# One DMA queue, known semaphores and chunk-wise stores in a scan kernel with a planned instruction order

## The chip, the cores and the metric

The kernel runs on one core of a Trainium2 chip. Its engines run side by side, each through its own list of instructions in order: TensorE (PE, with its weight loads as PEld), VectorE (DVE), ScalarE (ACT), GpSimd (POOL) and SyncE (SP), which computes nothing and here issues transfers. Engines wait for each other, and for transfers, by semaphores. The metric is the time of one execution on the device in microseconds (us); lower is better. Changes of about half a per cent can be told from none.

## The reference

The reference is a network of two blocks on an input of shape (4, 384, 32, 32). Each block is a state-space scan with projections, followed by a feed-forward part; the second one is a mixture of four experts, two of them per token. What matters here is the scan, and the vectors dt and dt u that it needs. For the first block:

```python
dts = jnp.einsum('bkrl,kdr->bkdl', dts, dt_projs_weight)
A = -jnp.exp(A_logs.astype(jnp.float32)).reshape(K, D, N)
dt = jax.nn.softplus(dts.astype(jnp.float32) + dt_projs_bias.astype(jnp.float32)[None, :, :, None])
...
def step(h, inp):
    dtt, ut, bt, ct = inp
    dA = jnp.exp(dtt[..., None] * A)
    h = h * dA + (dtt * ut)[..., None] * bt[:, :, None, :]
    y = jnp.einsum('bkdn,bkn->bkd', h, ct)
    return (h, y)
```

The second block has the same recurrence over 768 channels in one direction, with a convolution ahead of it and a gate behind it.

## The kernel before

**Passes, parts and steps.** The scans are cut into 48 passes: 32 of the first block (an image, a direction, a half of its 1024 positions), 16 of the second (an image, a half of the positions, a half of the channels). A pass has 384 channels and 512 positions. It has three parts of 128 channels, and a part has four steps `m`, each of which holds four of the 16 states: the 128 partitions are 32 channels by 4 states, and four tiles `x` of a step cover the part's channels. One step is: ScalarE makes the decays `da` = exp(dt A) (L1784, four instructions), GpSimd makes `s` = dt u times B for all four tiles (L1778), VectorE runs the four scans (L1793) and multiplies by C (L1842; a share of it goes to GpSimd, L1858), TensorE adds over the states into `acc` (L1814), and after each part VectorE adds `acc` into the output (`gather`, L666 to L672 and L918).

**How dt reaches its layout.** `prep_pass` (L522) makes dt and dt u of a whole pass as [128 channels, 3 chunks, 512 positions]: a matmul with `dtw` (L529), a softplus on ScalarE (L540 to L560), a sum on TensorE (L553) or VectorE (L562), and a multiply by u on GpSimd (L568). `spread_out` (L511) stores the result into a DRAM buffer in four transfers, a quarter of the partitions each, for all three chunks together: once for dt after its last chunk, once for dt u after its last chunk, 384 transfers of 192 KB in all, all on SyncE's queue. `spread_pass` (L575) loads it back for each part with each row repeated over four partitions: dt u in one load of 1024 KB (L590, on SyncE's queue, two buffers `dtus`) and dt in two loads of 512 KB (L596, on ScalarE's queue, three buffers `dts`). The second half of a part's dt goes into the buffer that the first half of the part before held, so it can be issued only when the decays of that part's last step on tiles 0 and 1 are done. `bt` and `ct` hold the rows of B and C repeated over the partitions (L1775, SyncE's queue); these rows come from DRAM buffers that `rows_out` (L491, ScalarE's queue, L494) writes.

**How a new quad starts.** Two passes share one projection, a quad. `ask_quad0` (L648) loads its small weights `wx0` and `dtw` (L651, L652) as soon as the preparation of an earlier pass that uses `dtw` is over; `prep_quad0` (L627) projects on TensorE (L637), ScalarE copies the result to `xd` (L642), and the rows for B and C are stored.

**What sets the order.** Nothing is scheduled by the compiler. A planner in the kernel (`Plan`, `Lane`, `Op`) goes through the work with estimated costs and writes the instructions out in the order of its own clock. The scans and what belongs to each step are fixed streams (`Op`); all else runs in lanes, generators that yield (engine, cost) and get the time at which it will be done. A lane's next request is ready when the one before it is done, unless it names another time. A transfer's cost is its estimated time to land, `land(kb)`; SyncE itself counts as occupied for 0.1 us by each. A transfer that is issued on ScalarE's queue takes 0.55 us of ScalarE in the plan (L595) or nothing (L494, L869). Lanes have ranks; passes come first, the experts last. Decisions of `choose` (L1951) also set how many of a step's multiplies by C VectorE leaves to GpSimd. The chip then runs each engine's list in the order written, with real waits.

**Semaphores of transfers.** The transfers of SyncE and ScalarE take eight semaphores in turn, in the order in which they are written out, whichever queue they go to. Before a transfer is issued, the one before it on the same semaphore must have landed. The planner does not know of this.

**The rest.** The gate's values `z` of the second block are stored from ScalarE's queue (L869) and loaded back (L929). The experts' weights stream through SyncE's queue into `mw` (L1355, 384 KB each), and the experts' matmuls (L1420, L1442) run on TensorE between the other work once tokens are routed (L1201). The last tokens are routed after the last scan, so that expert blocks are also what the kernel ends with.

Of the kernel before, what the change touches and what calls it, by code (L numbers as in the profile page):

```python
# [133 lines left out]

class Lane:
# [18 lines left out]
    def ready(self):  # L154
        return max(self.want[2] if len(self.want) > 2 else self.end, self.floor) + SLACK[self.rank >= LOW][self.want[0]]
# [11 lines left out]
class Plan:  # L167
# [39 lines left out]
    def mains(self, e):  # L207

        out = []
        for k in range(len(self.streams.get(e, ()))):  # L210
            op = self.head(e, k)
            if op is not None and all(d in self.end for d in op.deps):
                t = max([self.end[d] + LAG for d in op.deps], default=0.0) + op.lag
                out.append((max(self.free[e], t), k, op))
        return out
# [18 lines left out]
    def run(self):  # L234
        while True:
# [22 lines left out]
            start, what, e = best  # L258
            self.stuck = max(self.stuck, start)
# [4 lines left out]
            if isinstance(what, Lane):  # L264
                cost = what.want[1]
                self.free[e] = start + (0.1 if e == SP else cost - PITCH[e])
                what.end = start + cost - SOON[e]
                what.want = None
                Free.clock = what.end
                what.go(what.end, start)  # L270
            else:
                k, op = what
                self.at[e, k] += 1
                self.free[e] = start + (0.1 if e == SP else op.cost - PITCH[e])
                self.end[op.key] = start + op.cost - SOON[e]
                op.emit()


@with_exitstack
def layers(ctx, tc, ins, out, const):  # L280
# [160 lines left out]

    def layernorm(src, dst, eps, sq=None, sq_at=0.0, centred=False, scaled=True):
# [41 lines left out]
    def wload(src):  # L484

        w = yield from wts.take()
        yield SP, land(192) + 2.5
        nc.sync.dma_start(out=w.rearrange("p c m -> p (c m)"), in_=src)
        return w

    def rows_out(q, to):  # L491

        q["rows"] = q.get("rows") or dram.tile([2 * NS, L], F32, tag="rows", name="rows", bufs=4)
        nc.scalar.dma_start(out=q["rows"][:, to], in_=xd[q["at"] : q["at"] + 2 * NS, to])  # L494
# [12 lines left out]
    def load_dtw(q, k):  # L507

        nc.sync.dma_start(out=dtw[dt_rows(q), :], in_=ins["w_dt1"][:, k * D : (k + 1) * D])

    def spread_out(to, of):  # L511

        for q in range(NG):
            nc.sync.dma_start(out=to[:, :, q, :].rearrange("c r t -> r c t"), in_=of[q * QP : (q + 1) * QP])
# [5 lines left out]
    def prep_pass(v, p, of_u):  # L520
# [25 lines left out]
        if sums_on_pe(v):  # L546
            yield ACT, 1.5
            nc.scalar.activation(dtu, dtu, AF.Ln, bias=1.0)
            for c in range(NC):
                pd = yield from ps.take(True)  # L550
                yield PE, 2.0
                nc.tensor.matmul(pd, lhsT=ident, rhs=dt[:, c, :], start=True, stop=False)
                nc.tensor.matmul(pd, lhsT=ident, rhs=dtu[:, c, :], start=False, stop=True)  # L553
                yield ACT, 0.6
                nc.scalar.copy(dt[:, c, :], pd)
                ps.give(pd)
        for c in () if sums_on_pe(v) else range(NC):
# [6 lines left out]
        spread_out(spread[0], dt)  # L564
        for c in range(NC):
            yield POOL, 1.3 if len(of_u(dt[:, c, :], c)) == 1 else 1.75
            for (to, u), (by, _) in zip(of_u(dtu[:, c, :], c), of_u(dt[:, c, :], c)):
                nc.gpsimd.tensor_tensor(to, by, u[:, c], ALU.mult)  # L568
        tmp.give(dt)
        t = yield SP, land(768)  # L570
        spread_out(spread[1], dtu)
# [3 lines left out]
    def spread_pass(p):  # L575
# [3 lines left out]
        def gen():  # L579
            spread, stored = st.pop(("spread", p))  # L580
            for part in range(NC):
# [8 lines left out]
                nc.sync.dma_start(out=dtus[n % 2].rearrange("p q t -> p (q t)"), in_=of(1, 0, NG))  # L590
                plan.end["dtu", p, part] = plan.now + land(1024)
                for x in range(2):
                    m = 2 * n + x - 3
                    before = (yield from until(("da", 4 * (m // 2) + 3, 2 * (m % 2) + 1))) if m >= 0 else 0.0
                    yield ACT, 0.55, max(before, stored)  # L595
                    nc.scalar.dma_start(out=dts[(2 * n + x) % 3].rearrange("p q t -> p (q t)"), in_=of(0, 2 * x, 2))  # L596
# [5 lines left out]
    def prep0(b):  # L602
        u = st[("u0", b)]

        def ln(h):
            def gen():
                yield SP, land(768)
                nc.sync.dma_start(out=u[h], in_=half(x_in[b], h))
# [20 lines left out]
    def prep_quad0(q, b, k):  # L629
        def gen():  # L630
# [9 lines left out]
            for h in range(NT):  # L640
                yield ACT, 0.6
                nc.scalar.copy(xd[q["at"] : q["at"] + QROW + R0, cols(h)], px[h * HP : h * HP + QROW + R0])  # L642
            rows_out(q, slice(0, L))
            ps.give(px)
# [3 lines left out]
    def ask_quad0(q, k):  # L648
        def gen():
            yield SP, land(66)  # L650
            nc.sync.dma_start(out=wx0.rearrange("p c m -> p (c m)"), in_=ins["w_x0"][k])  # L651
            nc.sync.dma_start(out=dtw[dt_rows(q), :], in_=ins["w_dt0"][k])  # L652
# [21 lines left out]
    def post0(b, h):  # L674
# [15 lines left out]
        def add_x(c):  # L690
            def gen():
                xh = yield from t1.take()
                yield SP, land(256)
                nc.sync.dma_start(out=xh, in_=piece(x_in[b], c, h))
# [8 lines left out]
        def ln2():  # L703
# [8 lines left out]
            nc.sync.dma_start(out=fold[:, :, :32], in_=fold_d)  # L712
# [14 lines left out]
        def ffn(lane):  # L727
            def gen():
# [6 lines left out]
                for i in range(2 * lane, 2 * lane + 2):  # L735
                    w, proj1 = yield from wts.two()
                    yield SP, land(192) + 2.0
                    nc.sync.dma_start(
                        out=w.rearrange("p a m -> p (a m)")[zrow, :], in_=ins["w_fc1"][:, i * NC * P : (i + 1) * NC * P]
                    )  # L740
                    nc.sync.dma_start(
# [29 lines left out]
        def ffn_out():  # L771
# [4 lines left out]
            nc.sync.dma_start(out=spread.rearrange("p a m -> p (a m)"), in_=of)  # L776
# [12 lines left out]
            nc.sync.dma_start(out=half(x1[b], h), in_=y)  # L789
# [11 lines left out]
    def prep1(b, h):  # L801
# [6 lines left out]
        def conv(i):  # L808
            def gen():
                for j in range(NC):  # L810
# [8 lines left out]
                    nc.sync.dma_start(out=dg, in_=taps_d[c])  # L819
# [33 lines left out]
        def gate(i):  # L853
            def gen():
# [14 lines left out]
                nc.scalar.dma_start(out=to.rearrange("(c p) t -> p c t", p=P), in_=z)  # L869
# [16 lines left out]
    def prep_quad1(q, b, h):  # L886
        def gen():
# [3 lines left out]
            nc.sync.dma_start(out=wx1, in_=ins["w_x1"].rearrange("p (c m) -> p c m", c=NI))  # L891
# [12 lines left out]
            nc.scalar.copy(xd[q["at"] : q["at"] + QROW + R1, cols(h)], px[: QROW + R1])  # L904
            rows_out(q, cols(h))
            ps.give(px)
# [13 lines left out]
    def post1(b, h, early=False):  # L920
# [3 lines left out]
        def gate(i):  # L924
            def gen():
# [3 lines left out]
                nc.sync.dma_start(out=z, in_=of.rearrange("(c p) t -> p c t", p=P))  # L929
# [14 lines left out]
        def project():  # L944
            o = st["o", b, h] = yield from tmp.take()
            for m in range(NC):
                w = yield from wts.two()
                yield SP, land(384)
                for i in range(2):
                    nc.sync.dma_start(out=w[i], in_=w_out[m, :, i * NC : (i + 1) * NC])  # L950
# [20 lines left out]
        def add_x(m):  # L971
            def gen():
# [3 lines left out]
                nc.sync.dma_start(out=xh, in_=piece(x1[b], m, h))  # L976
# [12 lines left out]
        def end():  # L989
            o = st["o", b, h]  # L990
            t = yield SP, STORE
            nc.sync.dma_start(out=x2[b, h].rearrange("(c p) t -> p c t", p=P), in_=o)
# [16 lines left out]
    def centre():  # L1009
# [9 lines left out]
        for c in range(NI):  # L1019
# [7 lines left out]
            nc.sync.dma_start(out=taps_d[c], in_=dg)  # L1027
            t1.give(dg)
        plan.end["taps",] = plan.now
        for i in range(2):  # L1030
# [4 lines left out]
            nc.sync.dma_start(out=w, in_=ins["w_out"][i * D : (i + 1) * D].rearrange("(c p) m -> p c m", p=P))  # L1035
# [8 lines left out]
            for m in range(NC):  # L1044
                nc.sync.dma_start(out=out_d[m, :, i * NC : (i + 1) * NC], in_=w[:, :, m * P : (m + 1) * P])
            tmp.give(t)

    def zero():
# [4 lines left out]
        for slot in (*slot_x, *slot_y):  # L1053
            for x in range(slot.shape[0] // P // n):
                to = slot.rearrange("(n p) d -> p n d", p=P)[:, n * x : n * (x + 1), :]
                yield SP, 12.0
                nc.sync.dma_start(out=to, in_=rep(z[:, :D], n))
# [265 lines left out]
    def experts():  # L1323
# [21 lines left out]
        def weights():  # L1345

            for s, i in every:
# [4 lines left out]
                for q in range(2 * NQ):  # L1352
                    w = yield from mws.take()
                    yield SP, 0.1
                    nc.sync.dma_start(out=w, in_=of[q])  # L1355
                    wq.append((plan.now + land(393) + 1.0, w))

        def fetch():

            for n, (s, i) in enumerate(every):  # L1360
# [11 lines left out]
                nc.sync.dma_start(  # L1372
# [3 lines left out]
                nc.sync.dma_start(  # L1376
# [115 lines left out]
        def keep():  # L1492

            for s0, _ in every:
# [16 lines left out]
                for k in range(m):  # L1511
                    yield SP, land(192)
                    nc.sync.dma_start(out=slot_y[g % 3][bass.DynSlice(at + k * P, P)], in_=rows[k][:, :D])
# [6 lines left out]
    def combine(u):  # L1520
# [4 lines left out]
        def begin():  # L1525
            x = st["out", u] = yield from tmp.take()
            yield SP, land(768)
            nc.sync.dma_start(out=x, in_=x2[u].rearrange("(c p) t -> p c t", p=P))

        def some(j):  # L1530
            def gen():
# [10 lines left out]
                nc.sync.dma_start(out=b2, in_=ins["b2"])  # L1542
# [30 lines left out]
        def end():  # L1573
# [3 lines left out]
            nc.sync.dma_start(out=to, in_=x)  # L1577
# [3 lines left out]
        def early():  # L1581
# [3 lines left out]
            nc.sync.dma_start(out=b2[:NE, :D], in_=ins["b2"])  # L1585
# [9 lines left out]
        def by_rows(j):  # L1595
            def gen():
# [32 lines left out]
                nc.sync.dma_start(out=to, in_=part)  # L1629
# [143 lines left out]
    def load(p, m, of, to):  # L1773
        rows = passes[p]["q"]["rows"][of + 4 * m : of + 4 * m + 4, cols(passes[p]["h"])]
        nc.sync.dma_start(out=to[m], in_=rows.unsqueeze(0).to_broadcast([QP, 4, T]))  # L1775
# [211 lines left out]

    plan = Plan(
# [10 lines left out]
def land(kb):  # L1999

    return 3.5 + kb / 200
# [105 lines left out]
```

## Time and profile before

| what | value |
|---|---|
| three runs, median (lowest to highest) | 5049.6 us (5034.54 to 5051.74) |
| the profiled execution, its own time | 5032.81 us |
| its span in the profile | 5031.0 us |
| granted TensorE clock, mean | 0.894 |
| PE busy | 4262.9 us (85%) |
| DVE busy | 4159.0 us (83%) |
| ACT busy | 3037.3 us (60%) |
| POOL busy | 4006.4 us (80%) |
| moved by DMA | 899.33 MB, 179 GB/s |
| queue q1, the larger of the two hardware queues | 704.28 MB, 43.3% of 16 engines |
| queue q10, the smaller one | 166.22 MB, 9.7% |

The profile is one execution. Busy time counts an engine's computing instructions; the issue of a transfer and the wait for a semaphore are not busy time, but they stand in the timeline as instructions of the sequencer, named SPq or ACTq. A busy TensorE is not one at its peak, since matmuls are pipelined; 751.5 us of its busy time are small matmuls by zero (L1833) that the planner puts into its gaps. The idle time before an instruction is given with what ended it: "<-ACT da L1784" says that the last thing waited for was ScalarE's instruction of line 1784 that writes `da`.

### The profile page before, as it was taken

The numbers are of one execution on the slowest core, as the hardware profiler recorded it, in microseconds if no ns is written. First come the engines' busy times: TensorE is split into PE (matmuls) and PEld (weight loads), VectorE is DVE, ScalarE is ACT, GpSimd is POOL, SyncE is SP. The second block draws the span as 40 slices with busy tenths as digits, with TensorE's granted clock in tenths as the row PEclk, the third lists the DMA queues.
The fourth block names the chain that finished last, engine by engine and source line by source line (L and its number), as shares of the span: only waits on it lengthen the run. The fifth ranks groups of instructions, "written<-read, shape, count | busy, mean of one in ns | idle before, by whom it ended". The sixth has DMA issues, their size and how long they took to land. (4 is left out here: it accounts for less than half of the span.)

```text
span 5031.0 us, 57132 instructions
## 1 busy us (share of the span) xinstructions
PE 4262.9 (85%) x17967; PEld 2192.9 (44%) x17967; DVE 4159.0 (83%) x5754; ACT 3037.3 (60%) x4769; POOL 4006.4 (80%) x1826
## 2 busy tenths in 40 slices
PE   8777778887767799988877798899888888899999
PEld 3222222222223454444444454345534333569996
DVE  4999999999999899999989999999999999850002
ACT  4544458765545577767654577767685756554442
POOL 2999999999988898989988988889899988850002
PEclk9887889888888899999987899899988889899998
DMA  4344656654443565556564655466655454655556
GB/s 148 110 161 156 205 169 214 207 185 139 161 143 107 195 193 175 190 188 211 188 221 161 215 181 175 155 197 205 230 179 191 155 181 148 220 184 180 170 165 190
DMA packets 394191, 899.33 MB, mean 179 GB/s; under 512 B 62384, under 2 KB 143520, under 8 KB 375456
## 3 DMA queue, kind: packets, MB, share of 16 engines
q1 hardware_dynamic: 336672, 704.28, 43.3%
q10 hardware_dynamic: 49024, 166.22, 9.7%
q0 software_dynamic: 8192, 25.17, 1.6%
q8 instruction: 143, 2.34, 0.2%
q14 instruction: 160, 1.31, 0.1%
HBM read 712.11 MB, written 183.40 MB: 178 GB/s over the span
## 5 line engine op out<-in xcount | busy, mean ns | idle before, releaser
L1778 POOL TENSOR_TENSOR s<-dtus,bt 128x2048 f32<-128x2048 f32 x576 | 2605.3, 4533 | 178.1 <-PE acc L1814 67.2
L1784 ACT ACTIVATE da<-dts,a 128x512 f32<-128x512 f32 x2304 | 1530.2, 686 | 886.4 <-DVE s L1842 771.5
L1814 PE MATMUL acc<-s,four 128*32 128x512 f32 x4608 | 735.1, 682 | 382.0 <-POOL s L1858 344.9
L1858 POOL TENSOR_TENSOR s<-s,ct 128x512 f32<-128x512 f32 (+1 forms) x552 | 942.5, 1708 | 138.6 <-DVE s L1793 102.0
L1793 DVE TENSOR_TENSOR_SCAN da<-da,s 128x512 f32<-128x512 f32 x775 | 918.2, 1216 | 114.0 <-ACT da L1784 82.4
L1842 DVE TENSOR_TENSOR s<-da,ct 128x512 f32<-128x512 f32 x1529 | 1009.6, 680 | 0.1
L1793 DVE TENSOR_TENSOR_SCAN da<-da,state,s 128x512 f32<-128x512 f32 x754 | 939.5, 1277 | 17.7 <-ACT da L1784 10.1
L1833 PE MATMUL acc<-ident,few 128*32 128x256 f32 x2886 | 751.5, 416 | 36.2 <-DVE big L918 18.6
L1833 PEld LDWEIGHTS acc<-ident,few 128*32 128x32 f32 x2886 | 334.4, 119 | 510.6 <-issue 225.1
L1793 DVE TENSOR_TENSOR_SCAN s<-da,state,s 128x512 f32<-128x512 f32 x398 | 495.5, 1267 | 8.7 <-ACT da L1784 8.6
L1793 DVE TENSOR_TENSOR_SCAN s<-da,s 128x512 f32<-128x512 f32 x377 | 447.1, 1204 | 17.3 <-ACT da L1784 17.3
L1814 PEld LDWEIGHTS acc<-s,four 128*32 128x32 f32 x4608 | 106.5, 113 | 748.9 <-POOL s L1858 547.3
L1420 PE MATMUL ps<-tmp,mw 128*128 128x256 f32 (+1 forms) x1812 | 387.9, 369 | 22.3 <-ACT tmp L1465 11.5
L1442 PE MATMUL ps<-mw,tmp 128*128 128x192 f32 x2096 | 377.1, 337 | 17.5 <-DMA mw<-in_w_dram 6.8
L1442 PEld LDWEIGHTS ps<-mw,tmp 128*128 128x128 f32 x2096 | 350.4, 195 | 82.4 <-issue 42.9
L1420 PEld LDWEIGHTS ps<-tmp,mw 128*128 128x128 f32 x1812 | 316.5, 198 | 135.7 <-issue 30.4
L1615 DVE SCALAR_TENSOR_TENSOR big<-big,gk,da 128x384 f32<-128x384 f32 x2 | 1.2, 612 | 414.2 <-PE da L1613 414.2
L1605 POOL DMA_INDIRECT big<-ys,slot x12 | 11.8, 980 | 382.7 <-DMA ys<-t 379.3
L799 PE MATMUL ps<-big,w 128*128 128x512 f32 x576 | 280.2, 627 | 14.3 <-DMA w<-in_w_in_dram 8.2
L568 POOL TENSOR_TENSOR tmp<-tmp,big 128x256 f32<-128x256 f32 (+1 forms) x186 | 193.0, 1063 | 68.3 <-DVE tmp L1037 68.3
L529 PE MATMUL ps<-xd,dtw 12*128 12x512 f32 (+1 forms) x288 | 187.9, 743 | 17.2 <-ACT tmp L542 9.4
L838 PE MATMUL ps<-tmp,t 128*128 128x512 f32 x368 | 175.3, 620 | 15.6 <-ACT tmp L830 9.9
(448 smaller groups left out, 5322.2 us busy)
## 6 DMA issues: line engine op xcount, KB each, us to landing
mw<-in_w_dram SPq DMA_DIRECT2D x414, 384.0 KB
dts<-dts ACTq DMA_DIRECT2D x288, 512.0 KB
dtus<-dts SPq DMA_DIRECT2D x144, 1024.0 KB
dts<-tmp SPq DMA_DIRECT2D x376, 192.0 KB
bt<-rows SPq DMA_DIRECT2D x192, 256.0 KB
ct<-rows SPq DMA_DIRECT2D x192, 256.0 KB
dts<-in_w_dram SPq DMA_DIRECT2D x78, 384.0 KB
ys<-t SPq DMA_DIRECT2D x32, 768.0 KB
```

What stands on the lines that cost most here:

```text
L529: nc.tensor.matmul(pd, lhsT=dtw[dt_rows(q), c * P : (c + 1) * P], rhs=xd[dt_rows(q), cols(h)], start=True, stop=True,)
L568: nc.gpsimd.tensor_tensor(to, by, u[:, c], ALU.mult)
L799: nc.tensor.matmul(pi, lhsT=w[:, c, :], rhs=u[:, c], start=c == 0, stop=c == NC - 1)
L1420: nc.tensor.matmul(ph[:, k * width : (k + 1) * width], lhsT=w[:, c, k * P : (k + 1) * P], rhs=turned[:, c], start=c == 0, stop=c == NC - 1,)
L1442: nc.tensor.matmul(py[:, k * HD : (k + 1) * HD], lhsT=by_f(hids[half_], width)[:, at_, k * P : (k + 1) * P], rhs=w[:, f], start=4 * q + f ...
L1778: nc.gpsimd.tensor_tensor(ss[i % NSR], dtus[part_of(i) % 2], rep(bts[i % 4], NG), ALU.mult)
L1784: nc.scalar.activation(das[x], dts[(2 * part_of(i) + x // 2) % 3][:, x % 2, :], AF.Exp, scale=v["a"][:, g, m : m + 1])
L1793: nc.vector.tensor_tensor_scan(d if in_psum else s, d, s, 0.0 if v["first"] else state[:, v["slot"], j, x : x + 1], ALU.mult, ALU.add)
L1814: nc.tensor.matmul(acc[x * QP : (x + 1) * QP, :], lhsT=four, rhs=ss[i % NSR][:, x, :], start=m == 0, stop=m == 3)
L1833: nc.tensor.matmul(acc[:QP, : 2 * P], lhsT=nil.to_broadcast([P, QP]), rhs=rep(ident, 2), start=fresh, stop=fresh)
L1842: nc.vector.tensor_tensor(ss[i % NSR][:, x, :], das[x], cts[i % 4], ALU.mult)
L1858: nc.gpsimd.tensor_tensor(s[:, m:, :], s[:, m:, :], rep(cts[i % 4], NG - m), ALU.mult)
```

## The change

All transfers of SyncE and ScalarE go through SyncE's queue. Each is written out by a helper `ask`, which tells a new class `Ring` of its size. `Ring` keeps the time at which each of the eight semaphores will be free and the time at which the queue's data will have moved, at 220 KB per us; the planner lets SyncE start a transfer no earlier than the next semaphore is free, and counts SyncE as occupied for 0.55 us by each. `land(kb)` goes from 3.5 + kb/200 to 3.2 + kb/220. Transfers that were written on ScalarE's queue become steps of their lanes on SyncE, with their landing time as cost. `spread_out` stores one chunk of 128 channels (256 KB) in one transfer, and `prep_pass` calls it for each chunk as soon as dt or dt u of that chunk is made: 288 transfers of 256 KB in place of 384 of 192 KB. Where a store's step stands inside the lane of `prep_pass`, the lane's next request is ready when the store is estimated to have landed.

```diff
+class Ring:
+    at = busy = 0.0
+    lands = [0.0] * 8
+    n = 0
...
+    @classmethod
+    def next(cls):
+        return cls.lands[cls.n % 8] + 0.1
+
+    @classmethod
+    def issue(cls, kb):
+
+        t = max(cls.at, cls.next())
+        cls.busy = max(t + 1.2, cls.busy) + kb / RATE
+        cls.lands[cls.n % 8] = cls.busy + 1.0
+        cls.n += 1
+        cls.at = t + ISSUE
...
     def ready(self):
-        return max(self.want[2] if len(self.want) > 2 else self.end, self.floor) + SLACK[self.rank >= LOW][self.want[0]]
+        least = Ring.next() - LAG if self.want[0] == SP or len(self.want) > 3 else 0.0
+        return max(self.want[2] if len(self.want) > 2 else self.end, self.floor, least) + SLACK[self.rank >= LOW][self.want[0]]
...
-                out.append((max(self.free[e], t), k, op))
+                out.append((max(self.free[e], t, Ring.next() if e == SP else 0.0), k, op))
...
             start, what, e = best
+            Ring.at = start
...
                 what.go(what.end, start)
+                self.free[e] = max(self.free[e], Ring.at) if Ring.at > start else self.free[e]
...
                 op.emit()
+                if e == SP:
+                    self.free[e] = max(self.free[e], Ring.at)
...
+    def ask(queue, out, in_):
+
+        Ring.issue(int(np.prod(out.shape)) / 256)
+        queue.dma_start(out=out, in_=in_)
...
     def rows_out(q, to):
...
-        nc.scalar.dma_start(out=q["rows"][:, to], in_=xd[q["at"] : q["at"] + 2 * NS, to])
+        ask(nc.sync, out=q["rows"][:, to], in_=xd[q["at"] : q["at"] + 2 * NS, to])
...
-    def spread_out(to, of):
-
-        for q in range(NG):
-            nc.sync.dma_start(out=to[:, :, q, :].rearrange("c r t -> r c t"), in_=of[q * QP : (q + 1) * QP])
+    def spread_out(to, of, c):
+
+        ask(nc.sync, out=to[c].rearrange("r q t -> q r t"), in_=of[:, c])
...
                 nc.scalar.copy(dt[:, c, :], pd)
                 ps.give(pd)
+                yield SP, land(256)
+                spread_out(spread[0], dt, c)
...
             nc.vector.tensor_tensor(dt[:, c, :], dt[:, c, :], pd, ALU.add)
             ps.give(pd)
-        spread_out(spread[0], dt)
+            made = plan.free[DVE]
+            yield SP, land(256), made
+            spread_out(spread[0], dt, c)
...
                 nc.gpsimd.tensor_tensor(to, by, u[:, c], ALU.mult)
+            t = yield SP, land(256)
+            spread_out(spread[1], dtu, c)
         tmp.give(dt)
-        t = yield SP, land(768)
-        spread_out(spread[1], dtu)
         tmp.give(dtu)
...
-                    yield ACT, 0.55, max(before, stored)
-                    nc.scalar.dma_start(out=dts[(2 * n + x) % 3].rearrange("p q t -> p (q t)"), in_=of(0, 2 * x, 2))
+                    yield SP, land(512), max(before, stored)
+                    ask(nc.sync, out=dts[(2 * n + x) % 3].rearrange("p q t -> p (q t)"), in_=of(0, 2 * x, 2))
...
-                nc.scalar.dma_start(out=to.rearrange("(c p) t -> p c t", p=P), in_=z)
+                yield SP, land(768)
+                ask(nc.sync, out=to.rearrange("(c p) t -> p c t", p=P), in_=z)
...
+            ps.give(px)
+            yield SP, land(64)
             rows_out(q, cols(h))
-            ps.give(px)
...
 def land(kb):
 
-    return 3.5 + kb / 200
+    return 3.2 + kb / 220
+
+
+RATE, ISSUE = 220.0, 0.55
```

Every other `nc.sync.dma_start(...)` of the planned part becomes `ask(nc.sync, ...)` with the same operands.

## The prediction

> **What bounds the kernel now.** I read the stages first: busy time of each engine from the first scan (99.4 us) to the last (4478 us), and behind it. The columns are PE, PEld, DVE, ACT, POOL busy us, granted clock, DMA share, GB/s.
>
> ```profile
> 99.40:4478.00 4378.60, 3627.08 (x14812) 1691.00 (x14813) 4082.93 (x5460) 2767.76 (x4313) 3951.45 (x1769) 0.88 0.54 179
> 4478.00:5031.00 553.00, 545.63 (x2869) 465.17 (x2868) 43.11 (x126) 223.38 (x379) 44.41 (x44) 0.96 0.59 179
> ```
>
> In the first stage VectorE works 4083 of 4379 us: 296 us of idle time is all that a change in waiting can win there. In the last 553 us TensorE works without a gap on expert blocks whose tokens are routed late, so this stage moves with the first one as a whole. No transfer goes through ScalarE's queue there; I cost it at nothing (bounds -5 and +33 us, one block of 33 us more or less in the backlog).
>
> Then the waits, for who holds VectorE up and who stands behind that (total us, times, longest):
>
> ```profile
> ACT xd L642 <- PE ps L637: 106.8, 14, 15.7
> PE ps L637 <- DMA wx<-in_w_x_dram: 93.8, 12, 14.9
> DVE da L1793 <- ACT da L1784: 92.5, 39, 14.1
> ...
> DVE s L1793 <- ACT da L1784: 25.8, 13, 5.9
> ```
>
> The first two rows are one chain: the small weight `wx` (L651) lands late, the projection L637 stands first in TensorE's order and waits, ScalarE waits for its result and cannot make the decays behind it. The worst case, SyncE's timeline:
>
> ```profile
> 1662.24 0.54 SPq L1775 DMA_DIRECT2D bt<-rows  x1
> 1662.89 0.58 SPq L1775 DMA_DIRECT2D ct<-rows  x1
> 1663.53 0.59 SPq L590 DMA_DIRECT2D dtus<-dts  x1
> 1664.21 8.83 SPq L514 DMA_DIRECT2D dts<-tmp  x4
> 1673.09 0.43 SPq L651 DMA_DIRECT2D wx<-in_w_x_dram  x1
> ```
>
> and VectorE's line at the end of that chain:
>
> ```profile
> 1683.57 2.35 DVE L1793 TENSOR_TENSOR_SCAN da<-da,s 128x512 f32<-128x512 f32 x2 [14.12 <-ACT da L1784]
> ```
>
> The four quarter stores of dt u need 8.83 us although an issue takes 0.43: of the four, the third and the last wait, the last for 5.2 us, until the semaphore that a dts load from ScalarE's queue holds is free. Over the first stage I find 64 such waits of SyncE, 158 us, of which 132 us (46 waits) are for a dts load of ScalarE.
>
> **The change, part by part.** All times are on the profiled execution: 5032.8 us its own time, 5031.0 its span. Landings are read from the semaphores: the last increment before the semaphore's next transfer is issued.
>
> (a) *The wx chain.* Ten times a gap of VectorE ends a chain from L637: 4.8, 6.2, 9.9, 7.6, 5.9, 7.8, 14.1, 8.3, 7.3 and 5.0 us, 77 us together. Before these wx issues the trace shows 31 us of waits for a semaphore of ScalarE's loads, which the new order does not have, since semaphores are then taken in one queue's order and the eighth transfer back is some 20 us old (about 1800 transfers in 4379 us). One chunk store instead of four quarters ahead of wx saves 3 issues of 0.43 us each time, 13 us. The rest is GpSimd's multiply L568 being late and stays. I take -44 (bounds -77, all; 0, when GpSimd's lateness shows in full).
>
> (b) *Other gaps behind a late transfer* (1180, 2218, 3081, 3290, 4088, 4296 us): 29 us, of which a foreign semaphore is shown for 3.1 us in one, and ScalarE's table loads ahead of a dts issue for some 3 in another. With realistic issue times in the planner a little more: -9 (bounds -29 and 0).
>
> (c) *Start-up.* The last quarter store before the first pass waits 5.1 us for such a semaphore, and the first dtus load follows it directly: -5 (bounds -10 and +10, see f).
>
> (d) *ScalarE.* 328 issues leave it, 168 us (288 dts loads at 0.521 us by the row below). It is 37% idle in the stage, so most is hidden; of VectorE's waits for it, 119 us in all, 55 belong to (a); of the other 64 I take the share of its work that goes, 168/(2768+168) = 6%: -4 (bounds -64 and 0).
>
> ```profile
> L514 SPq DMA_DIRECT2D dts<-tmp x376: 302/432/1625, 72.7 to 4312.0; - x188
> L596 ACTq DMA_DIRECT2D dts<-dts x288: 520/521/2263, 80.2 to 4439.9; - x144
> L590 SPq DMA_DIRECT2D dtus<-dts x144: 512/525/1540, 89.8 to 4412.0; - x144
> ```
>
> SyncE gets the 168 us and loses 96 stores (41 us): +127 on 912 us of issuing and 3243 us of waiting in the stage. The waiting hides it; without that cover it costs 127.
>
> (e) *The dts loads in SyncE's queue.* This is the added wait. ScalarE issues the second half of a part's dt 0.25 us (mean) after the decay that frees its buffer; it lands 5.8 us later, and from there to the scan that needs it 5.75 us remain in the median (decay's own time off), 2.8 in the worst tenth. If all 144 landed later by d, and each kept its own slack, VectorE would lose 5 us at d = 2, 16 at 3, 42 at 4, 86 at 5, 149 at 6. In SyncE's queue the load can stand behind an instruction that still waits. The nearest rows: `bt` loads, issued there 0.2 us after their buffer is free, and dtus loads, 0.8 us late in the mean and over 3 us in a tenth of cases, against the later of buffer and predecessor. Drawing d from these rows plus half a us for sharing one ring gives 3 and 19 us; I take +10. The other end: at 72% of these moments SyncE stands in a wait; were each finished first (3.1 us mean, up to 26), it would cost 183. Behind a waiting dts load stand all other loads; dtus lands 20 us before its use and `bt` 23 in the median, so they bear it; wx does not, and this keeps (a) from its upper end. The 24 row stores and 16 z stores that also move (0.33 and 0.39 us) have no such user close behind.
>
> (f) *Chunk stores.* 384 quarter stores become 288 chunk stores. In the planner every store now stands inside the preparing lane, and all but the last add land(256) = 4.36 us before the next chunk: 5 x 4.36 = 21.8, less 7.3 - 4.4 = 2.9 for the smaller last store, 19 us a pass. No instruction waits for this on the chip; it sets the order. Preparation takes some 38 us (L529 to the last store) and in 43 of 48 passes lands over 20 us before the first load of its pass. At passes 0, 24, 26 and 46 it does not; there the cost is between 0 and 19 each, 76 in all. VectorE has nothing else then and few instructions get in between: +6.
>
> The new store writes [4, 32, 512] from 128 partitions. The only transfer here with an outer dimension of 4 on one side, `w<-spread_d` (192 KB), shows 5 semaphore increments where others show 16, and lands after 5.75 us (median of 8) against 3.75 for the 192 KB of `w<-in_w_in_dram`. So 2 us more for 36 KB more on each of the few engines; 256 KB gives some 52 KB more, +3 us, in which what follows in the ring waits: 288 x 3 = 860 us of these engines in 4379. For (e) that is a fifth of the loads by up to 3 us: it adds 1 to 4 us, inside the +10 taken.
>
> The Trainium skill, "DMA: Bandwidth & Descriptors", section on why a DMA increments its semaphore by 16, speaks against this store: it uses the largest number of engines up to 16 that divides the slowest dimension of both sides, so four. The trace agrees as far as its 5 increments tell. At the page's rate of about 27 GiB/s an engine, 64 KB each is an estimate of 2.3 us against 0.6 for 16 KB, 1.7 more a store where the row gives 3: 370 us less of these engines in all, and a sum lower by 1 or 2 us.
>
> **Sum.** -44 - 9 - 5 - 4 + 10 + 6 = -46: 4987 us for the profiled execution. The three runs' median, 5049.6, is 0.33% above it; 4987 becomes 5003.
>
> **Rivals.** *1, slower: dts behind SyncE's waits.* The moved loads come late because the planned order of releases by ScalarE and by GpSimd or TensorE does not hold. For: 72% of moments in a wait, slack of 2.8 us in the worst tenth. Against: `bt` loads lose 0.2 us. It decides from a mean delay of 4.3 us on, where the curve passes the 56 us of gains; at 5.5 us it costs 118, so 5049.6 + 118 - 56 + 6 = 5118; at 5, 5086.
> *2, slower: the preparation.* 76 us of (f) in full, and its 19 us also shift wx so that (a) keeps only its 13 us: 5049.6 + 76 + 10 - 13 - 18 = 5105. Against: stores land long before use in 43 passes.
> *3, faster by more.* With issue times and semaphores known, all of 77 + 29 us and the 5 go, and a tenth of the 64: -117, 4932. For: these are the gaps that a late transfer ends. Against: GpSimd's L568 is late in three of the ten cases.
> *4, no change.* wx still waits for the multiplies of GpSimd, so that (a) gives 10 us, and the dts loads cost their 19: 5049.6 - 10 - 18 + 19 + 6 = 5047. For: three of the ten cases. Against: the 31 us shown for semaphores.
>
> **How the numbers follow.** Forecast (4985 to 5024) 0.38; rival 1 0.27; rival 2 0.06; rival 3 0.17; rival 4 0.12. A measurement of this kernel tells about 0.5% from no change, 5024 to 5075. Faster: 0.38 + 0.17 = 0.55; same 0.12; slower 0.33. The range reaches into rival 3 and past the middle of rival 1: 4915 to 5125.
>
> **What would show it.** L637's wait for wx falls from 94 to below 50 us and the waits of VectorE's L1793 for the decays from 119 to 80 or less; no SyncE wait of over 2 us for a foreign semaphore is left; the chunk store shows 5 increments and lands at some 6 to 7 us. Rival 1: waits of ScalarE's L1784 for dts, now 35 us, rise over 150, and VectorE's for L1784 with them. Rival 2: gaps over 15 us at the scans that begin passes 24, 26 and 46. The last stage keeps its 553 us within 15. I am wrong in kind if VectorE's busy time itself moves by over 40 us, since the planner also deals out multiplies between VectorE and GpSimd.

## The result and the profile after

| | before | changed |
|---|---|---|
| median of 6 runs each, side by side | 5044.44 us (5033.91 to 5051.74) | 5069.04 us (5066.05 to 5077.6) |
| ratio, 95% interval | | 1.0056 [1.0044, 1.0069] |
| profiled execution: own time, span | 5032.81, 5031.0 us | 5066.85, 5065.0 us |
| granted TensorE clock, mean | 0.894 | 0.906 |
| VectorE in the scan stage: busy, idle | 4082.6, 292.0 us | 4069.8, 321.2 us |

The change costs 0.56%, and the forecast of 5003 us had the sign wrong. All medians and ratios here and below leave out one slow execution of a variant, e2, which took 5423.23 us at a granted clock of 0.722. The busy time by stages, with the same columns as in the prediction, the first line from the first scan to the last (the kernel before ends its last scan at 4474 us, and the table goes by that, not by the 4478 of the prediction):

```profile
102.20:4493.00 4390.80, 3595.20 (x14694) 1658.69 (x14693) 4069.64 (x5447) 2753.88 (x4306) 3959.12 (x1788) 0.90 0.54 178
4493.00:5065.00 572.00, 565.97 (x2977) 481.35 (x2975) 43.52 (x127) 236.81 (x398) 46.23 (x45) 0.96 0.59 180
```

VectorE does 13 us less work and idles 29 us more, so the scan stage is 16 us longer. It begins 2.8 us later (102.2 against 99.4). What follows the last scan grows from 557 to 572 us, because 26 expert blocks are done by then and not 27. Together 16.4 + 2.8 + 14.9 = 34 us, the difference of the two spans.

The waits of the kernel after (total us, times, longest), in the order in which the prediction read them:

```profile
ACT xd L681 <- PE ps L676: 128.7, 15, 13.2
PE ps L676 <- DMA wx<-in_w_x_dram: 87.9, 13, 9.9
DVE da L1835 <- ACT da L1826: 138.9, 60, 29.4
...
DVE s L1835 <- ACT da L1826: 37.9, 20, 6.8
ACT da L1826 <- DMA dts<-dts: 34.5, 18, 5.5
```

The projection (L637 before, L676 now) waits for `wx` as it did, 88 us against 94, and ScalarE behind it longer, 129 against 107. VectorE's wait for the decays is 138.9 us where it was 92.5, but 29.4 of this is the gap ahead of the very first scan, which the kernel before has too (23.6 us, put down to GpSimd). Yet the waits that were to free `wx` are gone: SyncE stood 143.7 us (49 times) before a transfer whose semaphore a load of ScalarE held, and 0 us after. The last row, ScalarE's wait for the moved dts loads, has not moved; in the kernel before it is

```profile
ACT da L1784 <- DMA dts<-dts: 35.0, 14, 6.5
```

So the loads that changed queue hold nobody up more than before, and `wx`, which was to be early, is late for a new reason. SyncE, TensorE, ScalarE and VectorE at one of its 16 loads (start, duration, engine, line, operation, tile; in brackets the idle time ahead and what ended it):

```profile
152.41 0.51 SPq L476 DMA_DIRECT2D dts<-tmp  x1
153.01 0.42 SPq L476 DMA_DIRECT2D wx<-in_w_x_dram  x1
...
159.67 4.22 PE L676 MATMUL ps<-big,wx 128*44 128x512 f32 x12 [7.80 <-DMA wx<-in_w_x_dram]
...
163.93 0.58 ACT L681 COPY xd<-ps 44x512 f32<-44x512 f32 x1 [7.96 <-PE ps L676]
...
165.13 1.22 DVE L1835 TENSOR_TENSOR_SCAN s<-da,s 128x512 f32<-128x512 f32 x1 [5.19 <-ACT da L1826]
```

All transfers are now written out by one helper, so they all have its line, L476. The request for `wx` leaves SyncE 0.6 us behind the last chunk store of dt u without a wait, but its matmul starts only 6.7 us after it. By the semaphores, in 14 of the 16 cases `wx` stands directly behind such a store, and in each of them it lands 0.18 to 0.21 us after the store does. A chunk store shows 5 increments (288 of 288) and lands after 6.91 us in the median (5.45 at least), a quarter store of before after 3.85. `wx`, 128 rows of 528 bytes, landed after 2.80 us in the median of its 16 loads and now takes 6.40.

### The profile page after: what moved, and what is told of

It reads as the page before. It is cut to its first block, busy times and chain, and to the rows that moved or that the text cites. A ratio compares the mean times of both kernels' runs of the same rounds, so it can differ in the third digit from the quotient of the medians.

```text
span 5065.0 us, 57171 instructions
## 1 busy us (share of the span) xinstructions
PE 4254.5 (84%) x17987; PEld 2179.4 (43%) x17987; DVE 4144.9 (82%) x5742; ACT 3029.4 (60%) x4771; POOL 4016.9 (79%) x1846
## 3 DMA queue, kind: packets, MB, share of 16 engines
q8 instruction: 143, 2.34, 0.2%
## 5 line engine op out<-in xcount | busy, mean ns | idle before, releaser
L1856 PE MATMUL acc<-s,four 128*32 128x512 f32 x4608 | 722.4, 672 | 373.8 <-POOL s L1900 332.0
L1484 PEld LDWEIGHTS ps<-mw,tmp 128*128 128x128 f32 x1928 | 321.7, 195 | 69.6 <-issue 45.1
L1484 PE MATMUL ps<-mw,tmp 128*128 128x192 f32 x1928 | 348.4, 337 | 2.7 <-ACT tmp L1530 1.9
L839 PE MATMUL ps<-big,w 128*128 128x512 f32 x576 | 296.4, 656 | 22.7 <-DMA w<-in_w_in_dram 13.2
L839 PEld LDWEIGHTS ps<-big,w 128*128 128x128 f32 x576 | 112.7, 207 | 193.6 <-issue 139.3
```

The lines of the kernel that those rows point to most:

```text
L839: nc.tensor.matmul(pi, lhsT=w[:, c, :], rhs=u[:, c], start=c == 0, stop=c == NC - 1)
L1484: nc.tensor.matmul(py[:, k * HD : (k + 1) * HD], lhsT=by_f(hids[half_], width)[:, at_, k * P : (k + 1) * P], rhs=w[:, f], start=4 * q + f ...
L1856: nc.tensor.matmul(acc[x * QP : (x + 1) * QP, :], lhsT=four, rhs=ss[i % NSR][:, x, :], start=m == 0, stop=m == 3)
```

## The experiments

The theory from this was that the narrow store costs by holding up what is asked for right behind it. Its rivals were the longer lane in the plan, the dts loads in SyncE's queue (rival 1 of the prediction), and a price that each store has wherever it stands. Ratios are to the kernel before on the same chip, which ran at 5045.25 us (e1 to e4), 5042.37 (e5 to e8) and 5041.2 (e9 to e12).

**e1: the same list of instructions, the store wide.** Each chunk store writes 128 rows of 2 KB in place of [4, 32, 512]. No instruction changes its place. The rows of dt and dt u then stand in another order, so other values are computed and other tokens may be routed; VectorE's 5742 instructions and the 2336 transfers are the same, in the same order.

```diff
-        ask(nc.sync, out=to[c].rearrange("r q t -> q r t"), in_=of[:, c])
+        ask(nc.sync, out=to[c].rearrange("r q t -> (r q) t"), in_=of[:, c])
```

> The changed kernel with one edit: a chunk is stored as [128, 512] into contiguous memory instead of [4, 32, 512]; the rows of dt and dt u stand in another order inside a chunk, so the result is another one, and every engine's list is the same, instruction by instruction. Narrow-store theory (a store on few engines holds up the small loads behind it): 16 increments, landing of a store about 4 us instead of 6.9 (median), of wx 3 instead of 6.3, the gaps of VectorE behind the projection of a quad fall from 84 to under 50 us, and the time by 30 to 60 us: 5010 to 5040, ratio to before 0.994 to 1.000. Order theory (what was lost came from the new order of instructions or from SyncE's queue, not from the store): within 10 us of the changed kernel, 5060 to 5080, ratio 1.003 to 1.007.

Measured: 4976.95 us, ratio 0.9865 [0.985, 0.988], 92 us below the changed kernel. The store shows 16 increments and lands after 2.78 us in the median, `wx` after 2.19. The waits, and then the same place in the timeline of e1:

```profile
ACT xd L681 <- PE ps L676: 69.7, 15, 8.9
PE ps L676 <- DMA wx<-in_w_x_dram: 36.1, 11, 6.9
```

```profile
152.63 0.32 SPq L476 DMA_DIRECT2D dts<-tmp  x1
153.05 0.38 SPq L476 DMA_DIRECT2D wx<-in_w_x_dram  x1
...
155.29 4.83 PE L676 MATMUL ps<-big,wx 128*44 128x512 f32 x12 [3.20 <-DMA wx<-in_w_x_dram]
...
161.36 1.22 DVE L1835 TENSOR_TENSOR_SCAN s<-da,s 128x512 f32<-128x512 f32 x1 [1.18 <-ACT da L1826]
```

The matmul starts 2.2 us after the request, and VectorE's gap at the end of the chain is 1.18 us where it was 5.19. Over the stage, VectorE's gaps behind the quads (those over 2 us beside a quad's projection) fall from 84.5 to 20.8 us (79.8 before the change), and its idle time outside them from 237 to 214. The order is the same in both kernels, so the form of the store alone is worth these 92 us.

**e2: the changed kernel with the quarter stores of before.** The four stores of dt, or of dt u, go out together once all three chunks are made, and the lane's steps for single chunks go with the chunk stores (not shown):

```diff
-        ask(nc.sync, out=to[c].rearrange("r q t -> q r t"), in_=of[:, c])
+        for q in range(NG):
+            ask(nc.sync, out=to[:, :, q, :].rearrange("c r t -> r c t"), in_=of[q * QP : (q + 1) * QP])
```

> The changed kernel with the quarter stores of before, four after the last chunk of dt and four after the last of dt u; queue, known semaphores and land() stay as changed. Narrow-store theory: all stores with 16 increments, landings back to some 4.7 us in the mean, 30 to 60 us less than the changed kernel, 5010 to 5040. Queue theory (dts loads in SyncE's queue are what costs): nothing gained, 5060 to 5080. Lane theory (19 us more of preparation a pass): gained mostly in the first pass and at passes 24, 26 and 46, 10 to 40 us.

Measured: 4982.38 us, ratio 0.9878 [0.9861, 0.9894], faster than both kernels. First scan at 88.95 us, quad gaps 46.5 us, 27 expert blocks by the last scan.

**e3: a shorter lane.** The stores stay narrow, but the lane of `prep_pass` goes on 0.1 us after each and does not count on its landing.

```diff
-                yield SP, land(256)
+                yield SP, 0.1
...
-            yield SP, land(256), made
+            yield SP, 0.1, made
...
-            t = yield SP, land(256)
+            t = land(256) + (yield SP, 0.1)
```

> The changed kernel, but the lane of prep_pass goes on 0.1 us after a chunk's store is issued instead of at its estimated landing; stores stay [4, 32, 512]. Lane theory: 15 to 40 us less than the changed kernel, most of it in the first pass (now 41 us of idle time of VectorE against 30 before) and at passes 24, 26, 46. Narrow-store theory: within 15 us of the changed kernel, or slower, since three narrow stores then follow each other closely; wx lands after 6 us or later.

Measured: 5097.47 us, ratio 1.0103 [1.0088, 1.0119], 28 us slower. The stores now come closer together and land after 8.44 us in the median; `wx` after 6.91 in the mean (6.40 in the changed kernel). The lane's spacing is not what costs; it keeps narrow stores apart.

**e4: the dts loads on ScalarE's queue again**, all else as changed.

```diff
-                    yield SP, land(512), max(before, stored)
-                    ask(nc.sync, out=dts[(2 * n + x) % 3].rearrange("p q t -> p (q t)"), in_=of(0, 2 * x, 2))
+                    yield ACT, 0.55, max(before, stored), 1
+                    ask(nc.scalar, out=dts[(2 * n + x) % 3].rearrange("p q t -> p (q t)"), in_=of(0, 2 * x, 2))
```

> The changed kernel, but the 288 dts loads are issued on ScalarE's queue again, where the planner lets them wait for the next semaphore too. Queue theory: 20 us or more gained, the slack of the second half's load from landing to scan goes up from 6.2 us in the mean. Narrow-store theory: nothing gained, within 15 us of the changed kernel; the waits of SyncE for a semaphore held by ScalarE's loads come back (144 us before, 0 in the changed kernel).

Measured: 5105.08 us, ratio 1.0125 [1.0109, 1.0141], 36 us slower. Taking the loads out of SyncE's queue wins nothing, so rival 1 of the prediction falls. What the move itself is worth is less clear: VectorE idles 34 us more than in the changed kernel (354.7 against 321.2), and one gap that the changed kernel lacks is larger than that:

```profile
2862.78 0.69 DVE L1884 TENSOR_TENSOR s<-da,ct 128x512 f32<-128x512 f32 x1 [36.41 <-DMA ct<-rows]
```

In e4's order this load of `ct` stands behind the row stores of a quad whose `wx` is late behind its narrow store; in the changed kernel it was asked for ahead of them. So the loss is one of the new order at least as much as one of the queue.

**e5 and e6: which stores.** A flag makes some of the chunk stores wide, the rest stay narrow, and no instruction moves. In e5 it is the third chunk of dt u in each pass (48 of 288 stores), the one `wx` stands behind; in e6 it is all three chunks of dt (144).

```diff
+        to = to[c].rearrange("r q t -> (r q) t") if wide else to[c].rearrange("r q t -> q r t")
+        ask(nc.sync, out=to, in_=of[:, c])
...
-            spread_out(spread[1], dtu, c)
+            spread_out(spread[1], dtu, c, c == NC - 1)
```

> The changed kernel, every instruction in its place, with one store of each pass (the third chunk of dt u, the one that stands 0.6 us ahead of wx in SyncE's queue) made wide, 128 rows of 2 KB, as in e1; 48 of the 288 chunk stores. The rows of those chunks are permuted, so the output differs. Theory A, the hold-up is paid by wx alone, which lands together with the narrow store ahead of it (6.9 us after its request less the 0.6 between them): wx lands in about 2.3 us, VectorE's gaps at the quads fall from 84 us to 20 to 30, and the time from 5069 to 4995 to 5020, two thirds of the 92 us that e1 gained. Rival B, each narrow store costs alike, 92 us / 288 = 0.32 us by its engines' time: 48 x 0.32 = 15 us, 5054 (5045 to 5060).

> The counterpart of e5: the 144 stores of dt are wide, the 144 of dt u stay narrow, order untouched (rows of dt permuted, output differs). Theory A: wx still lands in about 6.3 us, the quad gaps stay near 80, and at most the rest of e1's gain comes, 92 - 64 = 28 us: 5040 to 5069. Rival B: half of the stores, half of the gain, 5069 - 46 = 5023 (5010 to 5032).

Measured: e5 5006.6 us, ratio 0.9934 [0.992, 0.9947]; e6 5051.51 us, ratio 1.0018 [1.0007, 1.0029]. One store in six brings 62 of the 92 us, half of all stores 18. The wait for `wx` in e5, and then in e6 (both have the line one lower than the changed kernel):

```profile
ACT xd L682 <- PE ps L677: 82.9, 15, 11.4
PE ps L677 <- DMA wx<-in_w_x_dram: 48.3, 12, 9.5
```

```profile
ACT xd L682 <- PE ps L677: 131.9, 15, 13.5
PE ps L677 <- DMA wx<-in_w_x_dram: 92.0, 13, 11.4
```

With the store ahead of it wide, `wx` lands after 2.34 us in the median and the quad gaps are 39.5 us; with the others wide, it lands after 6.38 and they are 88.4. So 45 of e5's 62 us lie behind the quads; VectorE's idle time outside them also falls by 22 us (237 to 215), in many small pieces that were not followed. The price goes with what stands behind the store. An equal price for each store would have given 5054 and 5023, the wrong way round.

**e7: the narrow store alone, in the kernel before.** Three chunk transfers in place of the four quarters, at the same place.

```diff
-        for q in range(NG):
-            nc.sync.dma_start(out=to[:, :, q, :].rearrange("c r t -> r c t"), in_=of[q * QP : (q + 1) * QP])
+        for c in range(NC):
+            nc.sync.dma_start(out=to[c].rearrange("r q t -> q r t"), in_=of[:, c])
```

> The kernel before with one edit: each store of three chunks goes as three narrow transfers, one for each chunk (4 x 32 rows), in place of its four quarters, at the same place of the queue; correct, and one request fewer for each of 96 stores. Theory A, the narrow form costs by what stands behind it: three in a row share the same 4 engines, so the last lands some 5.5 + 2 x 4.5 = 14 us after the request and wx behind it likewise; the ten waits at the quads grow by about 10 us each and the time from 5045 to 5110 to 5190. Rival B, three transfers take different engines and land side by side in 6 to 7 us: wx 6 us, +3 us at ten quads and 0.3 us less at SyncE for each store: 5050 to 5090. Rival C, the form is harmless where the stores are together, 5030 to 5050.

Measured: 5263.19 us, ratio 1.0435 [1.0421, 1.0449], 221 us slower and past the upper end expected. Three stores in a row land one after the other: where one was already queued behind another, the spacing is 2.58 us in the median and never under 2.27, so successive stores share engines. `wx` lands after 10.77 us in the median, again 0.2 us behind the last of them. That is earlier than the 14 us of theory A, so its time, too low even so, was not built from the right pieces.

The largest of its waits that grew (92.5, 106.8 and 93.8 us in the kernel before):

```profile
DVE da L1793 <- ACT da L1784: 204.0, 55, 22.8
ACT xd L642 <- PE ps L637: 188.9, 16, 25.3
PE ps L637 <- DMA wx<-in_w_x_dram: 177.6, 12, 22.6
```

The same chain shows twice the wait at `wx`, but it does not carry the whole loss: of the 222 us that VectorE idles more in the stage (513.7 against 292.0), 81 lie beside the quads' projections and 140 elsewhere. Other loads queued behind such a train land late too, for instance the experts' inputs, first in e7 and then in the kernel before:

```profile
PE ps L1386 <- DMA tmp<-xs: 61.3, 13, 10.2
```

```profile
PE ps L1386 <- DMA tmp<-xs: 22.2, 8, 6.2
```

SyncE's waits for its own semaphores go from 24 to 170 us.

**e8 and e9: where e2's gain comes from.** e8 is e2 with a planner that does not know the semaphores; e9 is e2 with the edit of e4.

```diff
-        return cls.lands[cls.n % 8] + 0.1
+        return 0.0
```

> e2 (the changed kernel with the quarter stores of before) with a planner that no longer knows the eight semaphores (the next free one is always there), all transfers still in SyncE's queue. It tells what of e2's 60 us comes from knowing the semaphores and what from the one queue. Theory A, from the queue: ScalarE's transfers no longer take semaphores that SyncE needs (143.7 us of such waits before, none after), so the time stays within 15 us of e2, 4970 to 5000. Rival B, from the knowledge: SyncE's waits for its own semaphores grow from 53 us to over 90 and the time goes back to 5015 to 5060.

> e2 with the loads of dts on ScalarE's queue again: without the narrow store, what the one queue is worth. Theory A: e2's 60 us come mostly from the semaphores that ScalarE's transfers no longer take, so 5005 to 5045, SyncE's waits for them back at 40 us or more (47 in e4, 144 before). Rival B: the queue is worth nothing once the planner knows the semaphores: 4975 to 5000.

Measured: e8 4993.05 us, ratio 0.99 [0.9884, 0.9915], which overlaps with e2's; whether the knowledge is worth anything stays open. e9 5022.64 us, ratio 0.9968 [0.9957, 0.998]: 40 us of e2's gain go. e4 lost 36 us with narrow stores, but not in the same way. What SyncE waits for ScalarE's dts loads, in e9 and then in e4 (by the profile's count, which takes in a little more than the 143.7 us above):

```profile
SPq L476 <- DMA dts<-dts: 220.1, 60, 8.4
```

```profile
SPq L476 <- DMA dts<-dts: 7.8, 5, 3.1
```

So the two losses are near each other, but no one price of the move is shown.

**e10, e11 and e12: wx out of the store's way.** `ask_quad0` waits for a pass that reads the old `dtw`, and that pass ends with its last store. `wx` itself needs only the quad before. It is asked for on its own, in a lane `ask_wx0` (not shown) that starts as soon as that one is done; `dtw` stays where it was. e10 is this in the changed kernel, e11 in e2, e12 in the kernel before.

```diff
-            jobs.append((("ask", n), asked, p, ask_quad0(q, x)))
-            deps = deps + [("ask", n)]
+            jobs.append((("wx", n), asked[:1] if before else [], p, ask_wx0(q, x)))
+            jobs.append((("ask", n), asked, p, ask_quad0(q, x)))
+            deps = deps + [("wx", n), ("ask", n)]
```

> The changed kernel, narrow stores and all, with wx asked for on its own as soon as the quad before has read it, and no longer together with dtw behind the pass's last store. Theory A, the narrow store costs by the transfer asked for right behind it: with wx out of its way the quads' gaps fall from 84 us to 35 or less, their waits for wx from 88 to under 25, and the time from 5069 to 4985 to 5015, about as far as e5. Rival B, the store takes that time from whatever stands behind it (decays, the matmuls of preparation), or the quads wait for something else that is late by the same time: 5040 to 5075.

> e2 (quarter stores) with the early wx of e10; correct, meant as the best version. Theory A: e2's quad gaps, 46 us, fall to about 20, and the time from 4985 to 4950 to 4970. Rival B, the order of the plan changes as much as the gaps: 4970 to 5000.

> The kernel before with the early wx alone. It tells whether the ten waits of VectorE that the forecast gave to wx (77 us) can be had without the change. Theory A: wx asked for some 10 us earlier is there when the quad starts, quad gaps from 80 to 30 or less, 5045 to 4985 to 5010. Rival B, the quads wait for the pass and its store as well, and little is won: 5025 to 5050.

Measured: e10 4993.63 us, ratio 0.9907 [0.9891, 0.9922]; e11 4946.15 us, ratio 0.9818 [0.9804, 0.9832]; e12 4972.91 us, ratio 0.987 [0.9855, 0.9885]. No row for `wx` is left among the longest waits of these three, and the quad gaps are 3.8, 20.4 and 14.9 us (of the 20.4, 14.6 are one wait for `ct`). What ScalarE still waits for the projection in e11, and its scan stage with the rest behind it:

```profile
ACT xd L679 <- PE ps L674: 20.8, 9, 4.4
```

```profile
91.60:4382.20 4290.60, 3632.86 (x14919) 1696.61 (x14920) 4073.58 (x5448) 2764.60 (x4317) 3955.60 (x1769) 0.90 0.54 183
4382.20:4940.00 557.80, 550.86 (x2902) 469.19 (x2900) 43.44 (x127) 227.71 (x383) 46.15 (x45) 0.96 0.55 178
```

e11 is the fastest of all: VectorE's idle time in the stage is 217 us where the kernel before has 292. The gain that the forecast saw in `wx` could also be had without the change (e12, 68 us). Even with `wx` out of the way, narrow stores (e10) leave the kernel 47 us behind quarter stores (e11); the two orders differ as well, so these 47 us are not the stores' alone.

## Why the prediction failed

**The step that failed** is the last of (f): "For (e) that is a fifth of the loads by up to 3 us: it adds 1 to 4 us, inside the +10 taken." The price of one store was about right: 3 us more were put down, 4.2 came at `wx` (2.19 to 6.40 us). It was charged to the wrong transfers. The step looked for what might stand behind a store and counted only the dts loads, which have slack, at random. But part (a) had just placed `wx` directly behind a store in ten cases, with no slack at all. 14 loads by some 4 us make up to 59 us there; e5 measured 45 in those gaps and 62 in all. The whole price of the form is 92 us (e1), against 1 to 4 in the sum.

**(a), the wx chain.** The foreign semaphores did go, as stated, and `wx` is asked for earlier: 0.6 us after the end of GpSimd's last multiply, 4.8 before (means of the 14 loads). But it then takes 7.0 us to land where it took 3.2, and so is there 7.7 us after the multiply, 7.9 before: one part of the change took back what the other gave. With wide stores it is there after 3.5 us, and the gaps behind the quads fall by 59 us (79.8 to 20.8), more than the -44 taken and inside the bounds; with the narrow stores they rise by 5. What the semaphores alone are worth here is not shown: in e2 they are gone too, `wx` is there only after 8.9 us, and yet the gaps are down to 46.5, so the order of the plan moves them as well.

**(b), (d), (e).** VectorE's idle time outside the quads is 212 us before and 214 in e1, so these terms cancel there, as -9, -4 and +10 nearly did. In the changed kernel itself it is 237: 23 us of the narrow form's price lie here, which the sum had nowhere either. Of (e) itself: the second half of dt is issued 0.36 us after its buffer is free (0.25 before) and lands after 5.87 (5.84), so the +10 were not spent. The first half lands after 7.7 us (6.2), without more waiting of ScalarE. Kernels with the loads on ScalarE's queue are 36 and 40 us slower (e4, e9), by waits that differ.

**(c), start-up**, had the wrong sign: the first scan starts 2.8 us later, and VectorE idles 41 us where it was 30, from just ahead of that scan to the end of the first pass. Wide stores leave the start at 102.4 us; the shorter lane gives 97.5 (e3) and quarter stores 88.95 (e2), so here it is the planned order and not the form of the store. The planner's lane, +6 in (f), was to show at passes 24, 26 and 46 too; there no gap grew, and e3 is slower, not faster, with the lane shortened.

**The last stage**, costed at nothing (bounds -5 and +33), grew by 15, inside the bounds: one expert block fewer was done before the last scan. e1, e5, e6 and e10 have 26 blocks and the same 570 to 572 us; all others have 27 and 553 to 562. The former all have chunk-wise stores with the longer lane, but so has e4 with its 27; why the plan loses a block was not followed.

**The sum** of -46 describes e1 rather than the changed kernel: on profiled spans e1 is 55 us below before (4976.4 against 5031.0), in the medians 68.

**The rivals.** 1 fell with ScalarE's wait for dts (34.5 us, not over 150) and with e4; its sum also counts the 6 us of (f) twice (56 is already 62 - 6), so that 5118 should read 5112. 2 fell with the passes and with e3. 3 saw gaps that can be won: e11 wins 95 us, but by another edit. 4 gave (a) only 10 us because GpSimd's multiplies are late; e1 wins 59 at the quads without touching them. None had the store ahead of `wx`. That 5069 lies within the range, and even in the band taken for no change, is luck: the range reached that far for rivals 1 and 4, and neither was at work.

**The signs.** Right: no foreign semaphore is left, the store shows 5 increments and lands after 6.9 us, dts waits as before, VectorE's busy time moves by 13 us. Wrong: L637's wait for `wx` (88 us, not below 50), and VectorE's for the decays (177, or 147 without the gap ahead of the first scan, not 80 or less). The last stage, 557 to 572 us, is just at the 15 us allowed.

## What to carry to other kernels

A transfer that runs on few engines is paid for first of all by what is asked for right behind it in the queue, not by its own user and not by all alike: name that transfer and its slack before pricing the store. When one change both frees a waiting load and rewrites the transfer ahead of it, cost the two at the same place. A small load that many wait for should not hang on a condition that belongs to its neighbour; asked for by itself in the kernel before (e12), it gained 68 us, more than the 46 forecast for the whole change.

## What the runs showed of the hardware

**How narrow the store is.** With nothing else in flight (the store asked for at 143.3 us), the packets of the chunk store in the changed kernel are 128 of 2 KB, four of them in flight for 3.05 us of its 5.82; their times add up to 16.2 us, 4.0 for each of four engines. The wide store of e1 at the same place has 16 in flight, 11.2 us in all, 0.7 for each, and lands after 2.0 us.

**Which engines.** The landings of e7, 2.58 us apart, show that narrow stores in a row wait for each other, although three of them would need only 12 of the 16 engines. This agrees with the Trainium skill, "DMA: Bandwidth & Descriptors", section "Why a DMA increments its semaphore by 16 and not by 1": such a transfer takes the lowest-numbered engines, so always the same ones. The prediction drew only the number of engines from that section. The estimate from the page's rate, 2.3 us for each 64 KB, is near the spacing in a row (2.58) and below the 4.0 us of a store by itself.

**What stands behind it.** `wx` shows 16 increments and yet lands with the narrow store, 0.2 us later, in 14 cases of 14. Twelve of its increments have come 3.0 us after the request, the other four only from 5.1 us on (medians of the 14); in e1 the thirteenth follows 0.04 us after the twelfth. So its share on four engines waits for the store, and the load is complete only with it.
